# Layer 3's context keys and values, made in layers 1 and 2 and kept in DRAM

## The chip, the cores and the metric

The kernel is one program on one core of a Trainium2 chip. The metric is the device time of one execution in microseconds (us). Before the change the median of three runs is 2539.31 us (2538.98 to 2540.57).

The engines are named as the profile names them: PE multiplies matrices (PEld loads its weights), DVE and ACT work on tensors elementwise, POOL does the same and issues some transfers, SP issues most transfers. A DMA moves data between DRAM and the on-chip memory SBUF; results of PE land in banks of a second on-chip memory, PSUM, from which DVE or ACT must evacuate them to SBUF.

## The reference

The program is a perceiver of four layers. A latent array `x` of shape (2, 256, 256) passes three residual blocks in each layer: one over a context of shape (2, 4096, 256), one over itself, and one feed-forward block. Layers 0, 1 and 3 attend over the context; layer 2 reads it in another way. The context itself never changes.

The block whose work is moved is the context attention of layer 3. It has 16 query heads of width 16 and a single key head and a single value head, shared by all of them:

```python
def _L3_xattn_ref(q, kv, mem, w_q, w_kv, w_concat):
    c = jnp.concatenate([mem, kv], axis=1)
    qh = (q @ w_q).reshape(B, L, N_HEAD, D_HEAD).transpose(0, 2, 1, 3)
    kvp = c @ w_kv
    k, v = (kvp[..., :D_HEAD], kvp[..., D_HEAD:])
    attn_score = jnp.einsum('bhid,bjd->bhij', qh, k) / np.sqrt(D_HEAD)
    attn_prob = jax.nn.softmax(attn_score, axis=-1)
    out = jnp.einsum('bhij,bjd->bhid', attn_prob, v)
    ...
    return out @ w_concat

x = x + _L2_attn_ref(_layernorm(x), ...)
x = x + _L2_ffn_ref(_layernorm(x), ...)        # a second attention, then routed experts
x = x + _L3_xattn_ref(_layernorm(x), ctx_1024, ctx_1024, ...)
```

In the call both `kv` and `mem` are the context; every key and value then stands twice in the softmax, which gives the same result as once, so the kernel uses the 4096 context rows once. Layer 2's attention block is an attention with rotary positions; its feed-forward block holds a second attention and then routed experts. Keys `k` and values `v` depend on the context and on `w_kv` alone, not on `x`. They can be made at any time.

## The kernel before

The whole network is one program. `perceiver` calls one function per block: `l0_xattn`, `l0_attn`, `l0_ffn`, `l1_xattn`, `l1_attn`, `int8_and_conv` (layer 1's feed-forward and layer 2's context block together), `l2_attn`, `l2_ffn`, `l3_xattn`, `l3_attn`, `l3_ffn`. Everything is 32-bit floating point. A matmul instruction leaves two records in the profile.

**What sets the order.** Tiles of SBUF come from pools; a tile that is asked for where an older one lay waits until the older one's last reader or writer is done, a transfer included. The framework inserts these waits. Within an `in_order` block the instructions of the named engines are pinned to the order in which the Python code emits them, so the emission loops are a schedule written by hand. Weights go through one pool of four rotating buffers (`weight`, L315): a fifth weight's load waits for the last use of the first. The transfers that SP and ACT issue share eight completion semaphores, so each waits until the eighth before it has landed. PSUM is divided into banks with tags ("mm", "tr", "acc", "dec"), whose numbers `perceiver` sets for each block; in layer 2 there are 3 "mm", 3 "tr" and 2 "acc", in layer 3's context attention 4 "mm" and 4 "tr".

**Early pieces, already there.** Part of layer 1's context keys is made during `l0_attn` and `l0_ffn`. `early_open` (L903) makes a generator of pieces; `fill(n, tag, vector)` (L934) emits the next `n` pieces at the point where it is called. A piece is one matmul instruction of 128 x 512; two make a key block of 512 context rows, which ACT (or DVE, where `vector` is set) evacuates with its bias, and which a DMA writes to DRAM (L929 from ACT, L926 from POOL). `l1_xattn` reloads these blocks (L1127). `self_attention` (L789) takes `fill` as an argument. It runs 24 turns `k`: turn `k` computes maxima for `k` below 16 and exponentials (L840) of turn `k - 6`, weighs values in some turns, and calls `fill` once in each of the turns 0 to 21.

**Layer 1's context attention** (`l1_xattn`, L1069) is a pipeline over 128 units `g` that ends in a drain: the last weighing (L1208), sums over `total` from POOL (L1196), a reciprocal (L1245), the scaled result `zT` (L1249), the output projection. Then `l1_attn` starts and loads its input weight `win` (L1346).

**Layer 2's attentions.** `l2_attn` (L1800) makes queries, keys and values in `rope_front` (L681), with a small table of rotary positions loaded by SP (L686), and calls `self_attention` without `fill`. `l2_ffn` (L1812) starts with a norm of a norm, transposes to `hT`, projects, attends, transposes, projects (`linear`, L444). Then a second norm (L420 to L424) leads to `h2T` (L439), from which the router chooses experts for rows; rows are scattered to DRAM and the expert units follow.

**Layer 3's context attention** (`l3_xattn`, L2209). `keys(b)` loads the context of batch `b` in four chunks of 1 MB and returns twelve parts: eight `key` parts (a block of 512 columns: two matmuls, ACT evacuation L2239) and two each of `value` (L2248, L2253) and `turned` (L2258, L2259). Softmax needs the maximum of each row of scores first. The generator `maxima` multiplies queries and keys (L2286) and lets DVE reduce each bank (L2290). The front runs 18 double steps of it, that is 72 maxima, and the remaining 24 parts are woven in:

```python
                made.pop(0)()
                made.pop(0)()
                made += keys(1)
                steps = maxima()
                for _ in range(18):
                    next(steps)
                    next(steps)
                    if made:
                        made.pop(0)()
```

The main loop then runs over groups of heads and context blocks: scores again (L2314), exponentials (L2318), weighing (L2330), with the next group's maxima between. The four parts left over are made there.

## Time and profile before

| | us |
|---|---|
| median of three runs | 2539.31 |
| profiled execution | 2535.48 |
| its span | 2533.7 |
| PE busy in the span | 2422.4 |
| DVE busy | 1691.2 |
| ACT busy | 1350.2 |
| POOL busy | 908.7 |
| layer 1's drain, last weighing to first use of `win` | 1227.0 to 1247.8 |
| layer 2's first attention | 1543 to 1609 |
| layer 2's second norm and attention | 1609 to 1694 |
| its router and experts | 1694 to 1825 |
| layer 3's front, first to last double step | 1843.0 to 1903.6 |

Times within the execution are given from the start of its span. A line of a group gives: source line, engine, operation, output and input with shapes, how often; busy time and mean duration of one in ns; then the engine's idle time just before these instructions and what ended it. PE's matmuls are pipelined: a record of 592 ns is followed by the next 430 ns or less later, so a stretch is judged by its length and by busy time, not by adding durations. `PEclk` is the clock that PE was granted, as a share of full speed; over the whole execution it is 0.971. "Half clock" below means a stretch in which it is 0.5.

### The profile page before, as it was taken

The page shows a single profiled execution, that of the slowest core. Times are in us where ns is not written, and L with a number is a line of the kernel's source. Part 1 is how long each engine was busy: PE and PEld are TensorE (multiplying, and loading weights), DVE is VectorE, ACT ScalarE, POOL GpSimd, SP SyncE. Part 2 cuts the span into 40 slices and gives each one's busy share as a digit, 9 for nine tenths or more (in the row PEclk, how much of TensorE's full clock was granted, in tenths as well). Part 3 has the DMA queues.
Part 4 walks back from the last instruction along what each step waited for, and adds up shares of the span by engine and source line. Part 5 has one row for each costly group of instructions (what it writes and reads, how often), then busy time and mean ns, then how long its engine had stood idle before and what let it go on. Part 6 is the DMA issues. An engine that isn't in the chain of part 4 may idle for free.

```text
span 2533.7 us, 51186 instructions
## 1 busy us (share of the span) xinstructions
PE 2422.4 (96%) x20467; PEld 1624.6 (64%) x20469; DVE 1691.2 (67%) x3112; ACT 1350.2 (53%) x2554; POOL 908.7 (36%) x851
## 2 busy tenths in 40 slices
PE   8999999999999999999799999899899999999889
PEld 6855577777766666666533556558736666665678
DVE  5555588888877777777669655444367888844542
ACT  3334566666666666666566313342127777783512
POOL 0510066666666655556469221002101222200010
PEclk9999999999999999999899999879999999998889
DMA  7221433333342222223300100017620000004555
GB/s 298 96 96 67 136 101 101 98 96 93 106 121 70 74 68 68 68 70 93 108 9 1 67 21 26 26 35 288 251 75 18 2 2 2 2 2 163 189 235 215
DMA packets 86238, 231.39 MB, mean 91 GB/s; under 512 B 7369, under 2 KB 22417, under 8 KB 75505
## 3 DMA queue, kind: packets, MB, share of 16 engines
q1 hardware_dynamic: 77248, 212.13, 25.2%
q10 hardware_dynamic: 6624, 9.31, 1.0%
q0 software_dynamic: 2128, 6.69, 0.8%
q8 instruction: 161, 2.64, 0.4%
q14 instruction: 77, 0.62, 0.1%
HBM read 199.92 MB, written 28.18 MB: 90 GB/s over the span
## 4 chain that ended last, share of the span: by engine, by line
PE 44%; DVE 4%; ACT 2%; issue 1%; DMA 0%; DVEq 0%; ACTq 0%; SPq 0%
PE ps_mm L359 10%; PE ps_mm L2286 6%; PE ps_tr L2330 5%; PE ps_tr L2314 5%; PE ps_tr L359 3%; PE acc L359 3%; PE acc L1483 2%; PE ps_mm L817 2%; PE ps_mm L1442 1%; PE ps_tr L1442 1%; PE ps_tr L2449 1%; PE acc L858 1%; PE ps_tr L833 1%; PE ps_tr L2492 1%; PE acc L1700 1%
## 5 line engine op out<-in xcount | busy, mean ns | idle before, releaser
L1196 POOL TENSOR_TENSOR total<-total,S 128x512 f32<-128x512 f32 x434 | 542.8, 1283 | 227.8 <-ACT S L1185 227.3
L1185 ACT ACTIVATE S<-S 128x512 f32<-128x512 f32 x512 | 304.2, 626 | 209.8 <-DVE S L1182 209.6
L2290 DVE TENSOR_REDUCE mx<-ps_mm 128x1 f32<-128x512 f32 x512 | 317.9, 684 | 71.0 <-PE ps_tr L2314 53.9
L1171 DVE TENSOR_TENSOR most<-ps_mm,most 128x512 f32<-128x512 f32 x448 | 278.3, 684 | 100.8 <-ACT S L1168 100.8
L1182 DVE TENSOR_TENSOR S<-S,ps_dec 128x512 f32<-128x512 f32 x512 | 317.7, 681 | 1.7 <-PE ps_dec L1240 1.7
L1168 ACT COPY S<-ps_mm 128x512 f32<-128x512 f32 x512 | 262.2, 599 | 72.9 <-PE ps_mm L1161 72.9
L2318 ACT ACTIVATE PT<-ps_tr 128x512 f32<-128x512 f32 x476 | 246.8, 603 | 73.9 <-PE ps_tr L2314 71.5
L1114 PEld LDWEIGHTS ps_tr<-w_l1x_wv,ctxT 128*64 128x64 f32 x4096 | 235.5, 137 | 46.3 <-issue 41.6
L1161 PE MATMUL ps_mm<-qT,kT 64*128 64x256 f32 x2048 | 256.6, 389 | 0.7 <-DVE qT L1120 0.7
L1208 PE MATMUL acc<-S,v 128*64 128x256 f32 x2048 | 252.2, 385 | 1.7 <-ACT S L1185 1.0
L2286 PE MATMUL ps_mm<-kT,qT 32*128 32x512 f32 x1024 | 249.7, 617 | 0.2 <-DVE mx L2290 0.2
L1114 PE MATMUL ps_tr<-w_l1x_wv,ctxT 128*64 128x128 f32 x4096 | 248.3, 273 | 0.0
L2314 PE MATMUL ps_tr<-qm,kT 32*128 32x256 f32 x1904 | 238.3, 388 | 0.0
L1161 PEld LDWEIGHTS ps_mm<-qT,kT 64*128 64x128 f32 x2048 | 188.5, 186 | 44.4 <-issue 12.0
L1208 PEld LDWEIGHTS acc<-S,v 128*64 128x64 f32 x2048 | 139.5, 136 | 96.3 <-ACT S L1168 33.8
L1114 PE MATMUL ps_tr<-ctxT,w_l1x_wk 128*64 128x512 f32 x800 | 189.6, 593 | 0.0
L2314 PEld LDWEIGHTS ps_tr<-qm,kT 32*128 32x128 f32 x1904 | 171.0, 184 | 15.6 <-issue 6.2
L2339 POOL TENSOR_TENSOR sums<-sums,part 128x256 f32<-128x256 f32 x102 | 73.7, 723 | 256.8 <-ACT part L2338 256.8
L2330 PE MATMUL ps_tr<-PT,v 128*32 128x256 f32 x2048 | 139.4, 385 | 0.0
L2286 PEld LDWEIGHTS ps_mm<-kT,qT 32*128 32x128 f32 x1024 | 86.1, 184 | 60.6 <-issue 48.8
L336 DVE COPY v<-ps_tr 128x512 f32<-128x512 f32 x120 | 82.7, 689 | 42.3 <-PE ps_tr L1114 42.2
L1114 PEld LDWEIGHTS ps_tr<-ctxT,w_l1x_wk 128*64 128x64 f32 x800 | 59.7, 137 | 70.5 <-issue 58.9
(553 smaller groups left out, 3802.2 us busy)
## 6 DMA issues: line engine op xcount, KB each, us to landing
ctxT<-in_ctxT SPq DMA_DIRECT2D x144, 512.0 KB, 3.6
ctxT<-in_ctxT SPq DMA_DIRECT2D x16, 1024.0 KB, 6.3
w_l2f_gu<-in_l2f_gu SPq DMA_DIRECT2D x16, 1024.0 KB, 7.2
bd_dram<-bd SPq DMA_DIRECT2D x8, 1536.0 KB, 6.0
w_l3f_w<-in_l3f_w SPq DMA_DIRECT2D x11, 1028.0 KB, 8.4
w_l3f_w<-in_l3f_w SPq DMA_DIRECT2D x11, 1024.0 KB, 5.2
ctx<-in_ctx SPq DMA_DIRECT2D x8, 1024.0 KB, 4.8
w_l2f_down<-in_l2f_down SPq DMA_DIRECT2D x16, 512.0 KB, 3.8
```

What stands on the lines that cost most here:

```text
L359: self.nc.tensor.matmul(out, lhsT, rhs, start=i == 0, stop=i == len(pairs) - 1)
L1114: nc.tensor.matmul(ps[part], a[:, part], b, start=k == 0, stop=k == len(pairs) - 1)
L1161: nc.tensor.matmul(banks[hh, i][:, j, :], k[part, ts(2 * i + j, P)], q[u][part, :], start=True, stop=True)
L1171: nc.vector.tensor_tensor(m, ps, m, ALU.max)
L1182: nc.vector.tensor_tensor(t, t, spread[u][:, hh, :].unsqueeze(1).to_broadcast([P, 2, L]), ALU.add)
L1185: nc.scalar.activation(t, t, AF.Exp)
L1196: nc.gpsimd.tensor_add(tot, tot, t)
L1208: nc.tensor.matmul(av[u][part], vs[:, 2 * i + j, part], got[hh, i][:, j, :], start=g % 8 == 0 and i + j == 0, stop=g % 8 == 7 and i + j == 2,)
L2286: nc.tensor.matmul(ps, qT[rows, 2 * half + c, ts(t, P)], kT[rows, ts(j, 512)], start=True, stop=True,)
L2290: nc.vector.tensor_reduce(mx[:, c, r, j : j + 1], ps, AX.X, ALU.max)
L2314: nc.tensor.matmul(ps[:, i, :], kT[rows, ts(2 * u + i, P)], q[rows], start=True, stop=True)
L2330: nc.tensor.matmul(ps[ts(r, 32), :], v[:, 2 * u + i, :], pt[:, i, :], start=i == 0, stop=i == 1)
```

## The change

The sixteen key blocks and four value blocks of layer 3 are made earlier and kept in DRAM; `l3_xattn` reloads them.

- Layer 1's drain: `ahead_in_drain` makes the keys of batch 1, blocks 7 to 3, from context tiles that are still in SBUF; seven pieces after the last weighing, three before the last output. ACT evacuates and writes.
- Between layer 1 and 2: `ahead_fetch` loads the weights `l3x_wk` and `l3x_wv` and one 512 KB piece of context.
- Layer 2: `ahead_open` loads context in chunks of 1 MB (four buffers) and makes a generator with the remaining keys except two, and all values. It is called by `fill` in five kinds of places: two pieces before the transposes in `rope_front`; one in each of the turns 16 to 21 of `l2_attn`'s attention (evacuated by DVE, written by POOL); six before the transposes `hT`; one in each of the turns 0 to 5 (ACT) and 16 to 21 (DVE and POOL) of `l2_ffn`'s attention; the rest (a turn, a value, a turn) after the output projection.
- Layer 3: the keys of batch 1, blocks 1 and 2, from two 512 KB pieces loaded meanwhile, are made before the transposes of the normalised `x`.
- `l3_xattn` has no parts woven in any more. SP reloads 20 blocks of 256 KB. Its context loads (8 of 1 MB) are gone.
- The two weights leave the rotation of `weight`, so the next ones (`l3x_wq`, `l3x_wo`, `l3a_wr`, `l3a_rel`) are loaded one or two places earlier.
- The pools for all this live across blocks and lie apart from each other, so other pools' addresses move. `win` of `l1_attn` now lies over buffers of the drain, and the tiles made after `l2_ffn`'s attention over the context chunks.
- The transposes and the output projection of `l2_ffn` are pinned in order on PE, with the last `fill`.

```diff
-    def self_attention(self, pool, qT, kT, v, scale, rest=(), fill=None):
+    def self_attention(self, pool, qT, kT, v, scale, rest=(), fill=None, at=(range(6), range(6, 16), range(16, 22))):
...
+                    for steps, tag, vector in zip(at, ("tr", "acc", "mm"), (False, False, True)):
+                        if fill is not None and k in steps:
+                            fill(1, tag, vector)
...
+    def ahead_fetch(self):
+        self.ahead_wk, self.ahead_wv = self.ahead_weights(self.ahead_pool, "l3x_wk", "l3x_wv")
+        self.piece = self.ahead_pool.tile([P, KC, 512], F32, name="ahead_piece")
+        self.nc.sync.dma_start(self.piece, self.dram["ctxT"][:, 0, :, 0:512])
+
+    def ahead_out(self, pool, vector, key, ps, bias=None, order=lambda a: a):
+        nc = self.nc
+        t = pool.tile([P, 512], F32, name="ahead_t", tag="ahead_t")
+        if bias is None:
+            (nc.vector.tensor_copy if vector else nc.scalar.copy)(order(t), ps)
+        elif vector:
+            nc.vector.tensor_scalar_add(t, ps, bias)
+        else:
+            nc.scalar.activation(t, ps, AF.Identity, bias=bias)
+        if key is None:
+            return t
+        kept = self.ahead[key] = self.dr.tile([P, 512], F32, name="ahead_" + "_".join(map(str, key)))
+        (nc.gpsimd if vector else nc.scalar).dma_start(kept, t)
+
+    def ahead_key(self, pool, b, j, x):
+        wk = self.ahead_wk
+        tag, vector = yield
+        ps = self.bank([P, 512], tag)
+        for k in range(KC):
+            self.nc.tensor.matmul(ps, wk[:, k, :], x[:, k, :], start=k == 0, stop=k == KC - 1)
+            if k == 0:
+                tag, vector = yield
+        self.ahead_out(pool, vector, ("k", b, j), ps, self.col("lead"))
...
+    def ahead_in_drain(self, pool, ctx):
+        def parts():
+            for j in range(7, 2, -1):
+                yield from self.ahead_key(pool, 1, j, ctx[j])
+            yield
+        self.fill_from(parts())
+
+    def ahead_behind(self):
+        pool = self.behind
+        xs = {j: pool.tile([P, KC, 512], F32, name=f"behind_ctx{j}") for j in (1, 2)}
+        for j, x in xs.items():
+            self.nc.sync.dma_start(x, self.dram["ctxT"][:, 4 + j // 2, :, ts(j % 2, 512)])
...
+    def ahead_open(self, ctx):
+        pool = ctx.enter_context(self.tc.tile_pool(name="ahead", bufs=4))
...
+            have(2)
+            yield from self.ahead_key(pool, 0, 0, self.piece)
+            for c in range(0, 8, 2):
+                b, u = divmod(c // 2, 2)
+                for i in range(2):
+                    have(c + i + 3)
+                    for half in range(2):
+                        j = 2 * (c % 4 + i) + half
+                        if ("k", b, j) not in self.ahead and (b, j) not in ((1, 1), (1, 2)):
+                            yield from self.ahead_key(pool, b, j, cT[c + i][:, :, ts(half, 512)])
+...
             ahead = s.enter_context(self.tc.tile_pool(name="ahead_drain", bufs=2))
+                if g == G - 1:
+                    self.ahead_in_drain(ahead, {i % 8: ctx["v", i] for i in range(G - 5, G)})
+                    self.fill(7)
...
+                    if g - 11 == G - 1:
+                        self.fill(3)
...
-            qT, kT, v, rest = self.rope_front(pool, self.layernorm(x), wqk, wv, None, True)
-            z = self.self_attention(pool, qT, kT, v, 0.25, rest)
+            xn = self.layernorm(x)
+            qT, kT, v, rest = self.rope_front(pool, xn, wqk, wv, None, True, (2, 0, 0, 0, 0, 0))
+            z = self.self_attention(pool, qT, kT, v, 0.25, rest, self.fill, ((), (), range(16, 22)))
...
-                hT = self.to_T(self.norm_of_norm(x, 1e-6, x0), gain="norm1")
+                h = self.norm_of_norm(x, 1e-6, x0)
+                with self.in_order(mybir.EngineType.PE):
+                    self.fill(6)
+                    hT = self.to_T(h, gain="norm1")
...
-                z = self.self_attention(pool, qT, kT, v, 0.25)
-                zT = self.to_T(z, pool, "zT")
-                x1 = self.linear(zT, self.weight("l2f_wo"), x0, out=keep.tile([P, NT, D], F32, name="x1"))
+                z = self.self_attention(pool, qT, kT, v, 0.25, (), self.fill, (range(6), (), range(16, 22)))
+                with self.in_order(mybir.EngineType.PE):
+                    zT = self.to_T(z, pool, "zT")
+                    x1 = self.linear(zT, self.weight("l2f_wo"), x0, out=keep.tile([P, NT, D], F32, name="x1"))
+                    self.fill(48)
+            self.ahead_stack.close()
+            self.behind = self.behind_stack.enter_context(self.tc.tile_pool(name="behind", bufs=1))
+            self.behind_parts = self.ahead_behind()
...
+        xn = self.layernorm(x)
+        self.fill_from(self.behind_parts)
+        with self.in_order(mybir.EngineType.PE):
+            self.fill(4)
+            xnT = self.to_T(xn)
...
-                made.pop(0)()
-                made.pop(0)()
-                made += keys(1)
...
+                for j in range(8):
+                    nc.sync.dma_start(kT[:, ts(j, 512)], self.ahead["k", b, j])
+                for u in range(2):
+                    nc.sync.dma_start(v[:, u], self.ahead["v", b, u])
...
-                    if made:
-                        made.pop(0)()
```

## The prediction

> **What bounds the kernel now.** I read the page's totals first, then where PE's clock falls, then one table of stretches, then the groups and the order of work in each stretch that the change touches.
>
> ```profile
> span 2533.7 us, 51186 instructions
> PE 2422.4 (96%) x20467; PEld 1624.6 (64%) x20469; DVE 1691.2 (67%) x3112; ACT 1350.2 (53%) x2554; POOL 908.7 (36%) x851
> ...
> PE 44%; DVE 4%; ACT 2%; issue 1%; DMA 0%; DVEq 0%; ACTq 0%; SPq 0%
> ```
>
> PE works 96% of the span, so work moved elsewhere is paid again unless PE idles there. PE has to shed work where another engine can take over, or take it on where PE waits. The table says where that is (columns: stretch, length, each engine's busy time and instructions, PE's granted clock, DMA share, GB/s).
>
> ```profile
> core 0: us, PE busy (x) PEld busy (x) DVE busy (x) ACT busy (x) POOL busy (x), PEclk, DMA share, GB/s
> 1227.00:1241.00 14.00, 4.77 (x20) 2.20 (x20) 2.67 (x3) 0.89 (x3) 6.04 (x6) 0.74 0.00 0
> ...
> 1592.00:1604.00 12.00, 10.36 (x100) 6.64 (x92) 4.47 (x13) 7.16 (x14) 0.00 (x0) 1.00 0.01 1
> 1609.00:1620.00 11.00, 6.52 (x14) 3.44 (x15) 5.52 (x19) 2.89 (x7) 1.94 (x4) 0.53 0.00 0
> ...
> 1669.00:1682.40 13.40, 12.19 (x90) 7.41 (x89) 2.85 (x7) 7.07 (x14) 0.00 (x0) 0.81 0.00 1
> 1682.40:1694.40 12.00, 10.80 (x66) 6.54 (x64) 3.27 (x9) 3.76 (x10) 0.00 (x0) 0.78 0.00 0
> 1694.40:1705.00 10.60, 7.50 (x27) 5.74 (x28) 4.89 (x13) 2.07 (x5) 1.92 (x8) 0.66 0.60 198
> 1827.00:1843.00 16.00, 14.18 (x36) 6.82 (x36) 4.38 (x13) 2.65 (x5) 0.00 (x0) 0.79 0.68 275
> 1843.00:1903.60 60.60, 59.36 (x247) 21.24 (x246) 45.20 (x74) 12.16 (x18) 0.31 (x1) 1.00 0.19 71
> 1903.60:1954.00 50.40, 49.65 (x645) 31.61 (x648) 37.95 (x63) 39.22 (x81) 9.71 (x14) 1.00 0.07 23
> ```
>
> Layer 3's front (1843.0 to 1903.6) is full on PE, 59.4 of 60.6, with DVE 25% free. In layer 1's drain and around layer 2's norms PE idles and its clock is 0.53 to 0.78. The groups of the front say what PE does there:
>
> ```profile
> L2290 DVE TENSOR_REDUCE mx<-ps_mm 128x1 f32<-128x512 f32 x72 | 44.6, 684 | 16.4 <-PE ps_mm L2286 16.4
> L2286 PE MATMUL ps_mm<-kT,qT 32*128 32x512 f32 x146 | 29.2, 640 | 0.2 <-DVE mx L2290 0.2
> L359 PE MATMUL ps_tr<-ctxT,w_l3x_wk 128*128 128x512 f32 x57 | 28.4, 618 | 0.0
> ```
>
> DVE's 72 maxima wait 16.4 us for PE; half of PE's time makes keys.
>
> **The change, part by part** (minus is faster).
>
> *Layer 3's front.* 14 keys, two values and their turns leave it (14 x 1.72 + 2 x 1.92 + 2 x 0.66 = 29.2 us of PE; a key's four records start 0.43 us apart). What is late next is DVE: 72 maxima take 44.6 us, and the 222 ns reduction to the pad, the transposes and the sum behind it 1.9. 60.6 - 46.5 = 14.1 saved; bounds 12 (a reloaded key comes late) to 14.5. The 20 reloads of 256 KB go out from SP from 1824.7, where the context's loads stood; layer 1's reloads of this size (L1127) landed in 2.6 to 4.4 us, and a key is needed every 2.5 us: hidden.
>
> *Its lead-in.* Before, three keys cost 4.4 us of PE around the projection:
>
> ```profile
> 1828.82 2.10 PE L435 MATMUL ps_tr<-ident,xn 128*128 128x128 f32 x8 [6.52 <-DVE xn L384]
> 1830.71 1.92 PE L359 MATMUL ps_tr<-ctxT,w_l3x_wk 128*128 128x512 f32 x2
> 1832.42 8.03 PE L359 MATMUL ps_mm<-xT,w_l3x_wq 128*128 128x512 f32 x16
> 1840.28 2.74 PE L359 MATMUL ps_tr<-ctxT,w_l3x_wk 128*128 128x512 f32 x6
> 1842.95 1.14 PE L2286 MATMUL ps_mm<-kT,qT 32*128 32x512 f32 x8
> ```
>
> After, two keys (3.44) stand in the 6.5 us wait for the norm, starting at 1825.9 when the residual is complete, so the transposes start about 1829.4. The clock, half until 1834.4 before, should be up: projection 1832.1 to 1839.0, first maxima then instead of at 1842.95: -3.9. Bounds: -0.5 (half clock as before, the fill slow too) to -5.6. ACT's evacuation of the second key waits for the first's write, and the first query evacuation for the second's (about 1836, two writes at 2.0): slack, since four banks take the projection.
>
> *Its main loop* is PE's (49.65 of 50.4): two values and two turns less, 5.2 us of PE, -5.0; bounds -5.2 to -3. Layer 3 together: **-23.0**.
>
> *Layer 1's drain.* PE waits there:
>
> ```profile
> 1232.85 1.98 PE L359 MATMUL ps_mm<-total,ones 128*64 128x256 f32 x8 [5.87 <-POOL total L1196]
> ...
> 1240.63 0.34 SPq L1346 DMA_DIRECT2D win<-in_l1a_win  x1
> ```
>
> Seven half-keys (6.0 us) fill that wait, and the sums should run at full clock, 1.9 us sooner; the other three half-keys stand under the reciprocal (1.76). But the input weight `win`, released at 1240.6 and needed at 1247.8 (PE waited 2.2 for it), now lies over the drain's buffers: its load waits for two more evacuations and the last writes (2.0 each), about 1241.7, and SP has issued wk, wv, the 512 KB piece and three loads ahead of it. +1.0; bounds -1 to +2.5.
>
> *Layer 2's front.* Two half-keys in PE's 3.74 us wait; three 1 MB context loads go ahead of the rope table on SP (issued 1543.2, first used 1551.7; 8.5 us, and 3 MB at the 326 GB/s that the trace shows at 1241 to 1248 take 9.6 us). Clock up: as good as -1.5; table late: up to +3. I take 0. The Trainium skill ("TensorE: Matmul & The Clock Gate", section "What's actually happening") says that the clock rises only after a busy window of about 3.4 us: two half-keys of 0.86 would not make one, so by it no gain stands against the late table.
>
> *Attention in layer 2, turns 16 to 21.* One half-key per turn. Layer 0's attention has this already: its exponentials start 12.89 us apart from turn 16 to 21 (206.31 to 219.20), layer 2's 9.46 (1594.47 to 1603.93): 0.69 a piece, six pieces +4.1; bounds +3.4 to 6 x 0.86 = +5.2. The evacuations of these pieces are DVE's (0.75 each; it is busy 4.5 of 12 us there) and their writes POOL's (0.57 an issue; POOL is idle there), so both are covered; without that cover three of each would add 4.0.
>
> *Second half of layer 2, norm and attention.* Before the transposes six pieces (a value, its turn, three half-keys) fill PE, but two ACT evacuations (0.69, 0.58) and a write's issue move ahead of the square root, which delays the norm 2.0; half clock (1609.1 to 1619.4) would go, 2.5: -0.5, bounds -2.5 to +2. Turns 0 to 5: 13.0 us before, half of it at half clock; layer 2's first attention took 12.3 with its own extra work, plus pieces: 0, bounds -0.8 to +1.5. Turns 6 to 15: 19.7 before, 18.3 in the first attention at full clock, but an unfinished value holds one of three "tr" banks, 0 to 0.4 a turn: -0.5, bounds -1.4 to +2.2. Turns 16 to 21: 13.54 before, 11.46 + 3.43 = 14.9 after: +1.4, bounds +0.5 to +3. Behind them the clock stays up (6.3 us of last weighing against 3.8 in the first attention): -1.5, bounds -2.5 to 0.
>
> *After the output projection* (PE done 1694.33). A value copy (0.58) and a write's issue (0.33) come ahead of ACT's last square and table load: +1.0. The second turn waits for an ACT evacuation that stands behind the square root, and the norm's transposes stand behind that turn. The buffer of `h2T` lies over the freed context buffers, so its DVE evacuation waits for the landing of the last value's write:
>
> ```profile
> 1698.81 1.60 DVE L439 TENSOR_SCALAR h2T<-ps_tr,cols 128x512 f32<-128x512 f32 x2 [0.57 <-PE ps_tr L435]
> ```
>
> By these durations the copy ends at 1699.7, its issue at 1700.0, the write lands 2.0 later (median of layer 1's writes, L929): 1702.0, **+3.2**, and the router and everything behind it wait. POOL's tables and the clearing of the rows wait for it too (SP 1703 instead of 1695.4), ahead of a scatter that came at 1715.2 and would come at 1718: hidden. Bounds +1.0 (hidden by half-clock router time) to +4.5 (write 3.3). The Trainium skill ("DMA: Bandwidth & Descriptors", section "Anatomy of one DMA") puts a DMA at 2.0 us and its bytes at 436 GB/s, an estimated 2.6 us for 256 KB, in a fit made on another queue; the term would be +3.8.
>
> **Sum**: -23.0 + 1.0 + 0 + 4.1 - 0.5 + 0 - 0.5 + 1.4 - 1.5 + 3.2 = **-15.8**. The profiled execution took 2535.48 (span 2533.7 and 1.8 around it) and would take 2519.7; the median of the runs, 2539.31, stands 3.8 above it, so 2523.5. All bounds together give -30 to +8; they will not all fall one way, so -9 to -21 is the likeliest case's own range, 2518 to 2530. A measurement of this kernel can tell 0.2%, 5.1 us, from no change.
>
> **Rivals.** *The costs eat the gain* (same): upper bounds of the layer 2 and drain terms (2.5 + 3 + 5.2 + 2 + 1.5 + 2.2 + 3 + 0 + 4.5 = 23.9) against 23.0 give 2540. For it: each waiting engine has something queued behind. Against: they are separate waits. *Nothing is idle* (slower): one mechanism, every piece is paid in full where it is made, because PE's waits there only move back by the piece. 37.8 us of PE (16 x 1.72 + 4 x 2.58) against 23.0: +14.8, 2554. It decides from 28.1 of 37.8 on. For: PE is busy 0.86 to 0.91 in the turns. Against: layer 0 paid 0.69 of 0.86, and the drain and the norms show 5.9, 5.6 and 3.2 us of idle PE. *The clock gives more*: layer 2 and its norms hold about 48 us at half clock; were the lower bounds reached in its norm, turns and tail, 6 more, 2517. *The change does not do what it says*: the front's maxima were DVE's anyway; excluded by the 16.4 us that DVE waits.
>
> **Chances.** Likeliest 0.60, more gain 0.14, a smaller gain (-5 to -9) 0.08, all faster: 0.82. Same 0.10, slower 0.08. The range goes from 2513, under the clock's case, to 2538, over half of the same case, and leaves out about 0.15.
>
> **What would show it.** Front about 46.5 us with DVE without idle; first maxima about 4 us after where PE's projection ends less keys; exponentials of turns 16 to 21 about 0.7 a turn further apart; `h2T` about 3 us later from the projection's end; `win` landing about 1 us later from the drain's last weighing. I am wrong if the reloads stall the front's maxima, if `h2T` or `win` wait for more than a write, or if the pieces' clock does not hold.

## The result, and the profile after

The changed kernel takes 2547.20 us (median; 2546.81 to 2551.17) where the kernel before takes 2540.57 on the same chip (2537.59 to 2541.14). The ratio is 1.0031, with a 95% interval of 1.0021 to 1.0042: slower by 0.3%, against a forecast of 2523.5.

The profiled execution of after took 2548.09 (span 2546.3), that of before 2535.48, about 5 under its own median; so the two traces differ by 12.6, the medians by 6.6. Some 6 us of what the traces differ by therefore belong to these two executions and not to the change. The page of the kernel after begins like this:

```profile
span 2546.3 us, 51302 instructions
PE 2441.9 (96%) x20469; PEld 1642.9 (65%) x20469; DVE 1697.1 (67%) x3119; ACT 1344.0 (53%) x2547; POOL 911.3 (36%) x856
...
PE 90%; DVE 4%; ACT 3%; DMA 2%; issue 1%; SPq 0%; ACTq 0%; DVEq 0%
```

PE is shown 19.5 us busier with two matmul records more: some of them ran more slowly. The table of stretches, cut at the work that the one of before was cut at (1 to 24 us later) and around two new waits, says which (stretch, length, busy time of each engine with its instructions, PE's granted clock, DMA share, GB/s):

```profile
core 0: us, PE busy (x) PEld busy (x) DVE busy (x) ACT busy (x) POOL busy (x), PEclk, DMA share, GB/s
1228.00:1242.00 14.00, 13.83 (x54) 6.01 (x50) 3.03 (x4) 4.09 (x8) 7.66 (x6) 1.00 0.16 59
1242.00:1257.00 15.00, 3.10 (x10) 1.70 (x11) 4.14 (x13) 3.99 (x6) 0.63 (x2) 0.64 0.94 309
1553.40:1565.40 12.00, 9.57 (x30) 4.66 (x28) 3.11 (x7) 2.22 (x5) 2.18 (x13) 1.00 0.99 385
1658.00:1684.00 26.00, 24.13 (x175) 14.21 (x174) 12.27 (x20) 8.86 (x15) 0.00 (x0) 0.74 0.06 21
1684.00:1697.00 13.00, 12.36 (x129) 7.71 (x128) 8.46 (x16) 6.92 (x13) 0.00 (x0) 1.00 0.01 2
1697.00:1707.00 10.00, 10.00 (x83) 5.02 (x82) 2.34 (x4) 4.75 (x9) 1.08 (x2) 1.00 0.64 236
1707.00:1720.00 13.00, 11.98 (x104) 7.38 (x100) 5.65 (x12) 5.21 (x15) 0.00 (x0) 1.00 0.13 32
1852.00:1868.00 16.00, 15.05 (x36) 6.70 (x38) 5.04 (x17) 3.72 (x7) 0.56 (x2) 0.84 0.89 301
1867.30:1921.40 54.10, 52.22 (x159) 33.28 (x162) 47.07 (x77) 1.48 (x2) 0.31 (x1) 0.56 0.09 29
1921.40:1970.00 48.60, 48.60 (x647) 31.92 (x644) 41.19 (x68) 37.78 (x81) 10.42 (x15) 0.99 0.01 2
```

The drain's wait (first row) is filled and at full clock, as forecast. Directly behind it (second row) PE has 3.1 us of work in 15. Layer 3's front (1867.3) lost its 29 us of keys and shrank only from 60.6 to 54.1, at a clock of 0.56 where it had 1.00. Its groups:

```profile
L2396 PE MATMUL ps_mm<-kT,qT 32*128 32x512 f32 x148 | 52.4, 1053 | 1.5 <-DVE mx L2400 0.8 <-ACT qT L331 0.7
L2400 DVE TENSOR_REDUCE mx<-ps_mm 128x1 f32<-128x512 f32 x73 | 46.4, 686 | 6.1 <-PE ps_mm L2396 6.1
```

A record of the maxima's matmuls lasts 1053 ns where it lasted 640, and DVE, which should have set the pace, waits 6.1 us for PE.

Measured between the same instructions in both traces, the terms of the forecast became (minus is faster):

| term of the sum | forecast [bounds] | measured |
|---|---|---|
| layer 3's front, 1st to 72nd maximum | -14.1 [-14.5, -12] | -6.6 |
| its lead-in, router's end to 1st maximum (the experts included) | -3.9 [-5.6, -0.5] | -1.2 |
| its main loop, 72nd to 200th maximum | -5.0 [-5.2, -3] | -5.3 |
| layer 1's drain, to the first use of `win` | +1.0 [-1, +2.5] | +5.2 |
| layer 2's front, to the first exponentials | 0 [-1.5, +3] | +3.4 |
| attention, turns 16 to 21 | +4.1 [+3.4, +5.2] | +3.5 |
| second norm and its projections | -0.5 [-2.5, +2] | +1.0 |
| second attention, turns 0 to 5 | 0 [-0.8, +1.5] | +1.4 |
| turns 6 to 15 | -0.5 [-1.4, +2.2] | +6.2 |
| turns 16 to 21 | +1.4 [+0.5, +3] | +1.5 |
| last weighing and output projection | -1.5 [-2.5, 0] | -1.9 |
| to the evacuation into `h2T` | +3.2 [+1.0, +4.5] | +2.6 |
| router behind it | in no term | -1.2 |
| elsewhere | 0 | +4.0 |
| sum | -15.8 | +12.6 |

Of the 4.0 elsewhere, 1.1 has arisen by 13 us, and 1.7 comes from a half-clock window at 1191.5 in layer 1's attention, which several kernels have and several have not; both stand before any code that differs.

**Where the time went.** Four terms lie outside their bounds: front, drain, layer 2's front (by little) and turns 6 to 15; the main loop passes its lower bound by 0.1. The trace names a wait for two of them. In the drain, SP's queue waited for a write (waits of the kernel after; engine, line, what was waited for: us in total, times, longest):

```profile
SPq L1472 <- DMA ahead_k<-ahead_t: 4.2, 1, 4.2
```

SP in order of time, and PE's matmul behind it:

```profile
1241.65 0.43 SPq L947 DMA_DIRECT2D ahead_piece<-in_ctxT  x1
1242.24 0.48 SPq L1658 DMA_DIRECT2D l2x_pe<-in_l2x_pe  x1
1242.76 1.24 SPq L1658 DMA_DIRECT2D l2x_wp<-in_l2x_wp  x2
1248.32 0.33 SPq L1472 DMA_DIRECT2D win<-in_l1a_win  x1
...
1255.88 5.69 PE L359 MATMUL ps_mm<-xT,win 128*64 128x512 f32 x8 [8.72 <-DMA mat_b<-in_spread_b]
```

The last key's write, issued at 1242.52, landed 5.7 us later beside the loads just issued (the writes before it, at 1232 to 1241, took 2.0 to 2.6); only then could `win` go out, at 1248.32 where it went at 1240.63, and the matmul started 8.1 later than before (2.9 of it had arisen ahead of the drain). The last row names `mat_b`, which landed only at 1256.87; what the matmul reads is `win`.

In layer 2's front the rope table was late:

```profile
1556.99 0.69 DVE L333 COPY xT<-ps_tr 128x512 f32<-128x512 f32 x1 [0.86 <-PE ps_tr L435]
1565.77 0.69 DVE L715 TENSOR_TENSOR rt<-ps_mm,rope 128x512 f32<-128x512 f32 x1 [8.10 <-DMA rope<-in_rope]
```

It was issued at 1553.45, behind three context loads of 1 MB, and DVE, which waited for it, began 12.3 us later; before the change it landed in 2.9.

### The profile page after: what moved, and what is told of

The parts are those of the page before. It is cut to its first block, busy times and chain, and to the rows that moved or that the text cites. A ratio compares the mean times of both kernels' runs of the same rounds, so it can differ in the third digit from the quotient of the medians.

```text
span 2546.3 us, 51302 instructions
## 1 busy us (share of the span) xinstructions
PE 2441.9 (96%) x20469; PEld 1642.9 (65%) x20469; DVE 1697.1 (67%) x3119; ACT 1344.0 (53%) x2547; POOL 911.3 (36%) x856
## 4 chain that ended last, share of the span: by engine, by line
PE 90%; DVE 4%; ACT 3%; DMA 2%; issue 1%; SPq 0%; ACTq 0%; DVEq 0%
PE ps_tr L1232 15%; PE ps_mm L359 13%; PE ps_mm L1279 9%; PE acc L1326 9%; PE ps_mm L2396 6%; PE ps_tr L2440 5%; PE ps_tr L2424 5%; PE acc L359 3%; PE ps_tr L359 2%; PE acc L563 2%; PE acc L1609 2%; PE ps_mm L817 2%; PE ps_mm L1232 2%; PE ps_tr L833 1%; PE ps_mm L1568 1%
## 5 line engine op out<-in xcount | busy, mean ns | idle before, releaser
L2396 PE MATMUL ps_mm<-kT,qT 32*128 32x512 f32 x1024 | 273.1, 677 | 1.5 <-DVE mx L2400 0.8
L2424 PEld LDWEIGHTS ps_tr<-qm,kT 32*128 32x128 f32 x1904 | 172.1, 185 | 15.8 <-issue 6.2
L2396 PEld LDWEIGHTS ps_mm<-kT,qT 32*128 32x128 f32 x1024 | 109.1, 199 | 63.0 <-issue 41.4
```

The costliest lines, as they stand in the source:

```text
L2396: nc.tensor.matmul(ps, qT[rows, 2 * half + c, ts(t, P)], kT[rows, ts(j, 512)], start=True, stop=True,)
L2424: nc.tensor.matmul(ps[:, i, :], kT[rows, ts(2 * u + i, P)], q[rows], start=True, stop=True)
```

## The experiments

The first theory was four separate waits (late `win`, late rope table, the bank that an unfinished value holds, `h2T` over the outgoing tiles) and, largest, the clock of the front, with nothing to hold it once the keys were gone. The rivals were that transfers or DVE set those stretches anyway, and that PE is simply full. Unless said, each kernel is the changed kernel with one edit, executed once. Executions of one kernel differ by 4 to 10 us here, so these kernels are read by the stretch that the edit touches, and their total times alone show little.

**The rope table first.**

```diff
-            have(2)
+            self.after_rope = lambda: have(2)   # called behind the rope table's dma_start
```

> The changed kernel with the rope table's load issued ahead of the four context loads of 1 MB instead of behind three of them. Queue theory: the table landed 12.3 us after its issue because 3 MB stood ahead of it, and DVE waited 8.1 us for it; issued first it lands in 3 to 4 us and the first rotation follows the first projection, 5 to 6 us sooner, the whole 4 to 6 us shorter. Rival, something else is late just behind it (the values' evacuation, PE's clock, the contexts for the attention's pieces): less than 2 us.

2543.95 (before on that chip 2540.76). From the last transposes of the work ahead of layer 2's attention (L1712, L1586 before) to the first rotation 17.01 instead of 23.57 (18.43 before):

```profile
1555.91 0.69 DVE L334 COPY xT<-ps_tr 128x512 f32<-128x512 f32 x1 [0.86 <-PE ps_tr L436]
1558.13 0.69 DVE L718 TENSOR_TENSOR rt<-ps_mm,rope 128x512 f32<-128x512 f32 x1 [1.53 <-PE ps_mm L360]
```

DVE waits 1.53 for PE and no longer for the table, which landed 3.2 after its issue. Of the 6.6, 1.8 is given back before the first exponentials: 4.8 stay, more than the 3.4 that this stretch had cost; up to the first exponentials it is 1.4 shorter than before the change.

**The drain's tiles apart.**

```diff
-            ahead = s.enter_context(self.tc.tile_pool(name="ahead_drain", bufs=2))
             sp = s.enter_context(self.tc.tile_pool(name="l1x_s", bufs=40))
+            ahead = s.enter_context(self.tc.tile_pool(name="ahead_drain", bufs=2))
```

> The changed kernel with the pool of the drain's buffers opened last in layer 1's context attention, so that it lies at the top of SBUF, under tiles that layer 1's second block first uses some 20 us later, and the load of win waits for no write. Release theory: win was issued 7.7 us later than before because it waited for two writes that took 5.5 us beside 1.2 MB of loads; now it goes out within 2 us of the last output projection's end and lands some 7.5 us later: first matmul with win 5 to 6 us sooner than in the changed kernel. Rival, bandwidth: win lands behind the loads issued ahead of it anyway, 2 us gained or less.

2544.99 (before 2540.76). With the drain's tiles above the scores' buffers, the load of `win` waits for none of their writes; whether `win` itself had lain over them or only its pool is not shown. In this kernel's order of time:

```profile
1242.48 0.43 SPq L1472 DMA_DIRECT2D win<-in_l1a_win  x1
...
1251.65 6.29 PE L359 MATMUL ps_mm<-xT,win 128*64 128x512 f32 x8 [4.36 <-DMA win<-in_l1a_win]
```

Issued 5.8 sooner, and from the output projection to the matmul 9.50 instead of 13.97 (7.33 before). The rest, 2.2, is the load itself: its 1.7 MB land 9.0 after the issue, 7.0 before the change, with the new weights and the 512 KB context piece ahead of them.

**No unfinished value in turns 6 to 15.**

```diff
-                z = self.self_attention(pool, qT, kT, v, 0.25, (), self.fill, (range(6), (), range(16, 22)))
+                z = self.self_attention(pool, qT, kT, v, 0.25, (), self.fill, (range(5), (), range(16, 22)))
```

> The changed kernel with pieces in turns 0 to 4 instead of 0 to 5 of layer 2's second attention, so that no unfinished value holds one of the three tr banks in turns 6 to 15. Bank theory: the exponentials of turn 6 to turn 15, 27.9 us apart in the changed kernel (1667.3 to 1695.2) and 19.7 before, come back to 19 to 21. Rival, clock: PE runs at half clock from 1669.4 to 1683.0 whether or not a bank is held, and 24 to 27 us remain.

2545.53 (before 2540.22). Turns 6 to 15 took 18.29 instead of 25.91. ACT's exponentials in the kernel after, at half clock and then at full:

```profile
1671.96 1.09 ACT L840 ACTIVATE PT<-ps_tr 128x512 f32<-128x512 f32 x2 [1.67 <-PE ps_tr L833]
1675.54 1.08 ACT L840 ACTIVATE PT<-ps_tr 128x512 f32<-128x512 f32 x2 [2.49 <-PE ps_tr L833]
...
1683.82 1.08 ACT L840 ACTIVATE PT<-ps_tr 128x512 f32<-128x512 f32 x2 [0.85 <-PE ps_tr L833]
1685.75 1.08 ACT L840 ACTIVATE PT<-ps_tr 128x512 f32<-128x512 f32 x2 [0.84 <-PE ps_mm L817]
```

and in the edited kernel:

```profile
1677.03 1.09 ACT L840 ACTIVATE PT<-ps_tr 128x512 f32<-128x512 f32 x2 [0.48 <-PE ps_tr L833]
1678.54 1.08 ACT L840 ACTIVATE PT<-ps_tr 128x512 f32<-128x512 f32 x2 [0.43 <-PE ps_tr L833]
```

At full clock this turn takes 1.93 with the bank held and 1.51 without; other turns differ by up to 0.5 or not at all. But that is the smaller part: the half clock (1669.4 to 1683.0) is gone from this execution too, and that was not the bank's doing alone. Over all kernels here, the stretch's length against its time at half clock lies on two lines: eleven executions with the bank held (6.8 to 13.7 us at half clock: 22.99 to 25.96) on 20.1 + 0.43 per us; six without it (0 to 10.2: 18.29 to 22.73) on 18.1 + 0.44 per us. So of the 7.6 the bank is about 2.0 and the 13.6 us at half clock are about 5.8. Why the clock falls there for 0 to 13.7 us, from one kernel to another, stays open. The value left over adds 1.5 behind the output projection.

**The outgoing tiles apart from `h2T`.**

```diff
-        t = pool.tile([P, 512], F32, name="ahead_t", tag="ahead_t")
+        t = (self.ahead_outs or pool).tile([P, 512], F32, name="ahead_t", tag="ahead_t")
+        # ahead_outs: a pool of two such tiles, opened beside l2f_keep, that outlives the context buffers
```

> The changed kernel with the outgoing tiles of layer 2's pieces in a pool of their own (two buffers) that stays open, so that h2T lies over nothing that a write still reads. Theory: the wait for the last value's write after the output projection (7.05 us from its end to h2T's evacuation, 4.48 before) shrinks by the write's issue and landing, about 2.3 us, to 4.7 to 5.2; the rest is the value's copy ahead of the square root. Rival: the evacuation is held by PE's turn and the norm's transposes, not by the write: 6.5 or more.

2541.71 (before 2540.22). After, and then with the edit:

```profile
1725.31 1.41 DVE L439 TENSOR_SCALAR h2T<-ps_tr,cols 128x512 f32<-128x512 f32 x2 [2.68 <-DMA ahead_v<-ahead_t]
```

```profile
1723.14 1.41 DVE L440 TENSOR_SCALAR h2T<-ps_tr,cols 128x512 f32<-128x512 f32 x2 [0.42 <-PE ps_tr L436]
```

The wait for the write is gone: 5.06 instead of 7.05 after the output projection (4.48 before), and the router gained 1.3 more.

**The two keys of the lead-in earlier.** In the kernel after the keys start late and slow:

```profile
1851.78 6.33 PE L969 MATMUL ps_tr<-behind_ctx,ahead_l3x_wk 128*128 128x512 f32 x8 [3.67 <-DVE xres L2231]
1857.94 1.04 PE L435 MATMUL ps_tr<-ident,xn 128*128 128x128 f32 x8
1859.22 7.13 PE L359 MATMUL ps_mm<-xT,w_l3x_wq 128*128 128x512 f32 x16 [0.24 <-ACT xT L331]
```

They wait 3.67 us for a PSUM bank that the residual's evacuation frees, and take 6.33 instead of 3.44 at half clock (1850.3 to 1857.1).

```diff
             self.experts_in_turn(unit, n, kept, gather, ways, way, y)
+            self.fill_from(self.behind_parts)
+            with self.in_order(mybir.EngineType.PE):
+                self.fill(4, "mm")
```

(and the same lines taken out ahead of layer 3's transposes)

> The changed kernel with the last two keys emitted at the end of layer 2's experts, in a bank of that stage, instead of in layer 3 before the transposes. In the changed kernel these four pieces began at 1851.8 only, when DVE's last addition had freed the PSUM banks of the stage before, ran at half clock (1850.3 to 1857.1) and took 6.3 us, so the transposes started 3.3 us later than without them. Theory: now they run in PE's 3.7 us of idle time ahead of it and keep the clock up; from the router's first maximum (best) to the transposes 127.7 us become 123 to 125. Rival: the pieces are paid in full wherever they stand, 127 or more.

2547.58 (before 2540.22). The transposes came 1.7 sooner and the first maximum 1.2 later behind them, for the half clock now fell on the projection (1852.7 to 1859.6): 0.5 was gained.

**Unused work in the front.** Does the clock fall because the maxima alone are left, and is the front DVE's when it does not?

```diff
-                for _ in range(18):
+                for i in range(18):
                     next(steps)
                     next(steps)
+                    nc.tensor.matmul(self.bank([P, 512], "tr")[:, 0:C], self.ident, xnT[:, 0, 0:C], start=True, stop=True)
```

with C of 512, 256 and 128; the results are not used.

> The changed kernel with one matmul more in each of the 18 double steps of layer 3's front: 128 rows, 128 x 512, of the identity with the normalised x, into a bank that nobody reads (15.5 us of PE at full clock, useless work). Clock theory: after the change the front's maxima, which use 32 of PE's 128 rows, are all that PE does there; the profile shows clock 0.5 from 1874.2 to 1922.0 and one maximum every 0.74 us, so PE and not DVE bounds the front. With full-row work between them the clock stays at 1.0 and DVE bounds it: from the first to the 72nd maximum 46 to 48 us instead of 52.6, and the whole some 5 us shorter in spite of the added work. Rival, work counts: PE's rate is given and 18 x 0.86 to 18 x 1.7 us are added to what bounds the front: 68 us or more, the whole 15 to 30 us longer.

> As the run with useless work in layer 3's front, with 256 columns in place of 512 (18 x 0.43 = 7.7 us of PE at full clock). That run brought the clock back (0.5 only from 1869.7 to 1876.5) but took 54.75 us from the 1st to the 72nd maximum against 52.13 without it: its matmul stands in PE's queue behind four maxima that wait for banks, so the clock's gain was spent on the place. Clock-and-place theory: half the work holds the clock as well and costs PE half as much, 47 to 50 us. Rival, the clock follows the amount of full-row work: 256 columns are too few, the clock stays at 0.5 over most of the front, and it takes 53 to 58 us.

> As before with 128 columns (18 x 0.22 = 3.9 us of PE). Clock-and-place theory: if the clock holds, 45 to 47 us from the 1st to the 72nd maximum, DVE's own pace of 0.60 to 0.62 us. Rival, amount: half clock as in the changed kernel, 52 to 55 us.

2550.43 (before 2540.76), 2544.03 and 2557.32 (before 2540.22). With 512 and 256 columns the clock held for all but 6.8 and 3.4 us of the front, and it took 54.75 and 49.96; with 128 columns it fell at 1875.2 for good, and the front took 62.23, longer than either case of its expectation. So the clock is a cause, but the cure takes place of its own: 49.96 and not the 46.5 of DVE. I had put the fall down to the maxima's shape, 32 of the array's 128 rows. That can be tried with the same columns on 32 rows,

```diff
+                    nc.tensor.matmul(self.bank([P, 512], "tr")[:, 0:256], self.ident[0:32], xnT[0:32, 0, 0:256], start=True, stop=True)
```

and the amount against the length of one piece, with 128 columns on all rows after every single step (36 pieces).

> The changed kernel with 18 multiplications of 256 columns added in layer 3's front, one after every second step of the maxima, whose result is not used; they are as long as those that held the clock, but read 32 rows of the array where those read 128. If the clock falls in the front because the maxima keep only 32 of the 128 rows at work, these do not hold it: 0.5 through most of the front, front 55 to 60 us, whole kernel 2549 to 2556. If it falls because PE has gaps in time, or because there is too little of any other work, these hold it like the full rows: clock 0.95 or more, front about 50 us, whole kernel about 2544.

> The changed kernel with 36 unused multiplications of 128 columns and 128 rows in layer 3's front, one after every single step of the maxima: the same amount as 18 of 256 columns, in pieces half as long and half as far apart. If the amount of work on all rows decides, the clock holds (0.95 or more) and the front is 49 to 51 us, whole kernel about 2544. If the length of one piece decides, the clock falls to 0.5 as it did with 18 pieces of 128 columns, and the front is 58 us or more, whole kernel 2552 or more.

My theory fell: on 32 rows the clock held (half for 6.8 us at the end) and the kernel took 2542.95 with a front of 45.65, as fast as DVE can go (groups of its front):

```profile
L2396 PE MATMUL ps_mm<-kT,qT 32*128 32x512 f32 x144 | 44.4, 697 | 0.0
L2400 DVE TENSOR_REDUCE mx<-ps_mm 128x1 f32<-128x512 f32 x72 | 43.3, 677 | 1.8 <-PE ps_mm L2396 1.8
...
L2475 PE MATMUL ps_tr<-xT,ident 32*128 32x256 f32 x36 | 13.3, 451 | 0.0
```

DVE's wait is 1.8 us against 6.1. The 36 short pieces on all rows were far worse: 2592.88, half clock from 1869.7 through the whole front, 96.98 long, though PE was shown busy for 95.9 of 97.0 us. (Before on that chip: 2536.06.) Neither the rows nor the amount decides alone. What pieces on all rows do besides is seen in order of time; 256 columns on all rows, then on 32:

```profile
1879.54 0.59 PE L2396 MATMUL ps_mm<-kT,qT 32*128 32x512 f32 x1
1880.06 0.70 PE L2475 MATMUL ps_tr<-xT,ident 128*128 128x256 f32 x2
1880.69 2.16 PE L2396 MATMUL ps_mm<-kT,qT 32*128 32x512 f32 x8
1882.78 0.70 PE L2475 MATMUL ps_tr<-xT,ident 128*128 128x256 f32 x2
```

```profile
1879.85 1.95 PE L2396 MATMUL ps_mm<-kT,qT 32*128 32x512 f32 x6
1881.11 0.69 PE L2475 MATMUL ps_tr<-xT,ident 32*128 32x256 f32 x2
1881.64 1.35 PE L2396 MATMUL ps_mm<-kT,qT 32*128 32x512 f32 x4
```

The piece on all rows stands between the maxima, which start again 0.63 us after it began; the piece on 32 rows starts while maxima run, and they go on 0.53 later with no break. From one piece to the next it is 2.72 us in the first form and 2.39 in the second, where DVE, with four maxima at 0.60, sets the pace. The Trainium skill ("TensorE: Matmul & The Clock Gate", section "The mechanism") says that matmuls on different strips of 32 rows run at once in the array; the trace agrees: the piece on 32 rows begins at 1881.11, inside the maxima's 1879.85 to 1881.80. With the same 36 records the front takes 49.96 us in one form and 45.65 in the other.

Half as much on 32 rows (128 columns) brackets the amount:

> The changed kernel with 18 unused multiplications of 128 columns on 32 rows in layer 3's front, half as much as in f256_32rows. If the share of time in which some rows are at work decides with a threshold between the maxima alone and f256_32rows, either outcome is possible, and it brackets that threshold: held gives a front near 45 us and a kernel near 2542.5, fallen gives a front of 52 to 55 us and a kernel of 2547 to 2551. With 128 columns on all rows the clock fell; if these hold it, it is the place that the full rows take from the maxima, and not the amount, that lost it.

2547.47 (before 2541.14), front 50.34. The clock held for 16 us and then fell (two stretches of its front):

```profile
1867.50:1883.50 16.00, 16.00 (x72) 7.84 (x68) 15.93 (x27) 0.65 (x1) 0.00 (x0) 1.00 0.24 89
1883.50:1918.00 34.50, 32.94 (x116) 21.45 (x117) 29.16 (x48) 0.00 (x0) 0.31 (x1) 0.50 0.00 0
```

and the kernel after, with none of it, had held it for 7:

```profile
1867.30:1874.20 6.90, 6.90 (x25) 3.31 (x25) 6.73 (x12) 1.48 (x2) 0.00 (x0) 1.00 0.68 229
1874.20:1921.40 47.20, 45.32 (x136) 29.97 (x137) 40.34 (x66) 0.00 (x0) 0.31 (x1) 0.50 0.00 0
```

So with pieces on 32 rows the clock goes by their amount: in this loop, more than 128 columns and at most 256 for four maxima hold it. The column of PE's busy time doesn't show that amount: it is full in the 6.9 us before the fall. What the clock answers to in general stays open, since on all rows 256 columns in one piece held it and the same amount in two pieces did not.

**All of it together.** The four edits on the waits; then with 256 columns on all rows in the front; then with 256 columns on 32 rows.

> The changed kernel with four of its waits taken away together: rope table issued first, the drain's pool at the top of SBUF, no unfinished value over turns 6 to 15, outgoing tiles of layer 2 in a pool that stays. Theory: the changed kernel lost to these waits, each of which was a step of the prediction put too low; alone they gave 4.8 (rope), 3.9 (win), 6.3 (turns, net of a longer rest after the projection) and 2.5 us (h2T) in their places; together 15 to 18, so 2529 to 2533, 8 to 11 us under the kernel before. Rival: the places cover one another (what is saved early is waited for later, at the experts' weights or the clock), and less than half of it, 8, arrives: 2539 or more, as before.

> The same with 18 useless full-row matmuls of 256 columns in layer 3's front, which alone held the clock there (0.5 for 3.4 us instead of 47.8) and shortened the stretch from the 1st to the 72nd maximum from 52.1 to 50.0 us. Clock theory: 2 to 3 us less than the run without them. Rival, chance of where the clock's changes fall: no difference beyond 1 us.

> The four waits removed as in bcdh_waits_gone (2531.2 us), and the 18 unused multiplications of 256 columns on 32 rows in layer 3's front. If what is left of the gap to the forecast is the front's clock, the front falls from 52.6 to about 45.7 us as it did with these multiplications alone, nothing is given back later, and the kernel takes 2523 to 2526 us. If layer 3's main loop gives part of it back, as it did with the full rows (+1.9), 2526 to 2528. If the clock's fall hides other waits that come out when it is gone, 2530.

The first took 2531.21 (before 2539.76): 0.9969, interval 0.9959 to 0.9978. Against the kernel before, 6.6 us slower became 8.5 faster: 15.2 of the 17.5 that the four edits gave in their places. With full rows 2531.23: 0.9969, 0.9957 to 0.9981; its front gained 2.6 and the main loop gave 1.9 back. With 32 rows 2528.52 (before 2541.14): 0.9955, 0.9942 to 0.9969; its front took 45.31 and the main loop 95.44, nothing given back. The 2523 to 2526 expected did not come: between the two traces the front gives 7.3, but 3.6 are lost ahead of layer 1's drain, where the two kernels are alike, and 1.9 behind layer 3's last maximum.

**Work of use in the front.** The keys of batch 1 stay in the front, from their own context pieces, in pieces of 256 columns between the double steps; the drain's part goes, since it made them, and the edits on rope table, value and outgoing tiles stay.

```diff
+                def pieces():
+                    for j in own:
+                        ps = self.bank([P, 512], "tr")
+                        for at in range(0, 512, 256):
+                            for k in range(KC):
+                                nc.tensor.matmul(
+                                    ps[:, at : at + 256], wk[:, k, :], cT[j][:, k, at : at + 256],
+                                    start=k == 0, stop=k == KC - 1,
+                                )
+                                ...
+                                yield
```

with `own` 3 to 7, and then 1 to 7 and nothing ahead of layer 3's transposes.

> Five keys fewer are moved: batch 1's keys 3 to 7 are made in layer 3's front from their own context again, in pieces of 256 columns spread over the 18 double steps, instead of in layer 1's drain, which is as before the change. Rope first, whole values and the outgoing tiles as in the runs before it. Theory: PE has room there, since DVE's 72 maxima need 44.6 us and PE's 31, and real work holds the clock as well as useless work; the drain's cost (win 6 us late) is gone. Front 50 to 53 us, first matmul with win about 7.3 us after the last output projection as before the change; 2523 to 2530. Rival: pieces in the front stretch it by what they cost (8.6 us): front 58 or more, 2532 or more.

> As own5_in_front with batch 1's keys 1 and 2 in the front too and nothing before layer 3's transposes. Theory: the transposes start 3 us sooner after the experts; projection at half clock costs back 2; the front, with 12.0 us of pieces beside 31 us of maxima, takes 52 to 55; total within 3 us of own5_in_front. Rival: the two keys before the transposes were free, and the front pays for them in full: 3 us or more slower.

Five keys: 2527.70 (before 2539.76), 0.9952, 0.9939 to 0.9965. Seven: 2532.27, 0.9965, 0.9951 to 0.9979; its runs go from 2525.03 to 2533.83, so the two are not clearly apart. The front with five keys, in the columns of the table of stretches:

```profile
1850.20:1900.50 50.30, 48.67 (x183) 20.82 (x179) 44.44 (x74) 2.75 (x4) 0.31 (x1) 0.97 0.13 47
```

With five the front took 50.20 at full clock but for 3.4 us, 2.4 less than without them, and `win` was used 7.21 after the output projection, as before the change. Five keys are 8.6 us of PE, and they are free twice: the front, 50.20, is shorter than without them at half clock (52.59), and the drain no longer stands in `win`'s way. They are not free against a front whose clock is held by the pieces on 32 rows: 45.31. Seven cost 2.9 more in the front. The version with five is faster than the kernel before and does no unused work.

## Why the prediction was wrong

The sum was right in most of what moving PE's work costs, and wrong in the front that was left behind and in waits that the moved work brought. From the forecast -15.8 to the traces' +12.6 it is 28.4 us: the front makes 7.5 of it, turns 6 to 15 6.7, the drain 4.2, layer 2's front 3.4, the lead-in 2.7, and what no term held 2.8.

- *Wrong: "60.6 - 46.5 = 14.1 saved; bounds 12 (a reloaded key comes late) to 14.5."* DVE does go that fast: 45.65 and 45.31 where the clock held. But the step took PE's time for a maximum as fixed when the keys went, and bounded only the reloads. Left alone, the maxima lose the clock after 7 us, PE is busy 0.72 us for each (52.4 for 73) where DVE is 0.64 (46.4), and the front takes 52.1. I named the clock of the pieces as a risk, and not that of the stretch they leave. The rule of the Trainium skill that I cited ("TensorE: Matmul & The Clock Gate", section "What's actually happening") lets the clock rise after a busy window of 3.4 us; here it stayed at 0.5 for 47 us in which PE is shown busy for 45.3, so the rule can't be applied to the busy time of the records.
- *Wrong: "+1.0; bounds -1 to +2.5" for the drain.* The wait for the last write was named, and priced at 2.0, the median of layer 1's writes. The filled sums gained 1.5 and `win` lost 6.6: the last write landed 5.7 us after its issue, beside loads at 309 GB/s. The trace of before had such a case: the last of those 25 writes, issued at 268.6 behind four context loads, took 6.1. The Trainium skill's fit for such a write, an estimated 2.6 us, which I gave for `h2T` ("DMA: Bandwidth & Descriptors", section "Anatomy of one DMA"), agrees with the write issued at 1241.38 (2.6); for the one that decides here, issued 1.1 later beside the loads, the trace's 5.7 stands against it, and the write that `h2T` waited for, issued at 1723.18, took 2.0.
- *Wrong: "Clock up: as good as -1.5; table late: up to +3. I take 0."* Both effects were there, but a sooner use only lengthens the wait for a late table, so they may not be set against each other. I compared the table's landing with the 8.5 us that it had before its use, and put 9.6 for 3 MB where 12.3 passed. Three issues put it 1.3 later, and the full clock brought its use 1.4 nearer: with the table in time the use would have come 17.0 after the transposes, 5.8 after the issue. Issued first, it turns +3.4 into -1.4, close to the lower bound. My use of the skill's rule was beside the point: the clock did not have to rise, since it had not fallen here (1.00 from 1553.4 to 1565.4; before the change it was 0.5 from 1547.7 to 1551.1).
- *Wrong: "an unfinished value holds one of three "tr" banks, 0 to 0.4 a turn: -0.5".* The bank cost 0.4 to 0.5 in the turns where it showed, about 2.0 in all, within its bounds. What failed is the full clock of the first attention that the step took over: 13.6 us of these turns ran at half clock where 4.4 had before. Why it falls there stays open.
- *Wrong in size: the lead-in, -3.9, measured -1.2.* It lay between the bounds: "half clock as before, the fill slow too" is what happened to the fill, which also started 3.67 us late for a PSUM bank. (The eight key records shown before the change are two keys, not three; no term rests on that.)
- *Right:* the main loop (-5.3), the pieces in turns 16 to 21 of both attentions (+3.5 and +1.5; 0.58 a piece against 0.69), the last weighing (-1.9), and `h2T` (+2.6, with the write that I named). The norm (+1.0) and turns 0 to 5 (+1.4) lay at the upper parts of their bounds.

Of the rivals, "the costs eat the gain" has the right places; its waits were indeed separate, and two of them and the clock went past their upper bounds. "Nothing is idle" is excluded: a piece cost 0.58 of its 0.86 in the first attention's turns, and with the waits gone and the clock held the kernel gains 11 to 13 us (0.9955 and 0.9952), some three quarters of the forecast 15.8.

## What to carry to other kernels

When PE's work is taken out of a stretch, price what remains there at the clock that it can hold alone: the big filler may have been what kept the small matmuls fast, and it can be better to leave some of it there (here five keys made the front 2.4 shorter than none, seven 0.5 longer). When buffers are moved, look for the first load whose pool takes over their region, and for small loads behind large ones on the same queue: they cost 6.6 and 4.8 us here, where the matmuls hidden in these places were 8.6 and 1.7. A bound on a wait has to include the transfer's time under the load that the change itself adds.

## What the runs showed of the hardware

- Matmuls of 32 rows and 512 columns, one for each 0.60 us, don't hold the clock: it fell to 0.5 within 7 us and stayed there for 47, PE being shown busy for 45.3 of them. Eighteen more matmuls of 256 columns on 32 rows hold it, eighteen of 128 hold it for 16 us. Why it did not come back at half speed, when DVE waited for PE, stays open. The stretches at half clock named here come in steps of 3.4 us (3.4, 6.8, 10.2, 13.6, 47.8).
- The same columns cost 4.3 us more on all rows than on 32 (front 49.96 and 45.65), and 36 pieces of 128 columns on all rows, at half clock, made the front 97 us long.
- A write of 256 KB landed 2.0 us after its issue with no loads under way, and 5.7 us after it beside 1.2 MB of loads; the 16 KB rope table landed 12.3 us after its issue behind 3 MB, and in 2.9 to 3.2 with no context load ahead.
